# Router and low-rank columns appended to the weight blocks, all seven products joint, weight sums kept in DRAM

## The chip, the cores and the metric

One core of one Trainium2 chip runs the whole kernel. The metric is the device time of one execution in microseconds (us), the median of several runs. TensorE (PE in the profile) multiplies, VectorE is DVE, ScalarE is ACT, GpSimd is POOL, and SyncE (SP) issues every DMA of this kernel from one queue, in order.

## The reference

`x` is 8 batches of 1024 tokens with 1024 features, all float32.

```python
x = x + xattn(layernorm(x), ctx, mask)     # ctx: 64 memory rows per batch
x = x + ffn(layernorm(x), W, lora_A, lora_B, router_w)

def ffn(h, ...):                           # 8 experts, rank 16, top 2
    base   = h @ W.T                       # 1024 x 1024
    logits = h @ router_w.T                # 8 columns
    w      = top-2 softmax of logits, spread over 8 experts
    Ax     = h @ lora_A                    # 8 * 16 = 128 columns
    return base + 2.0 * ((Ax * w) @ lora_B)
```

So each token needs the 1024 x 1024 product, 136 more columns of the same input (128 low-rank, 8 router), a top-2 choice among 8 logits, and a product of 128 x 1024 that depends on that choice.

## The kernel before

The 8192 tokens are 64 tiles of 128, taken as 32 *pairs* (256 tokens); two pairs make a *quad*. `first()` handles pairs 0 and 1, loads the weights and forms sums of them; then `quad(u)` runs for u = 2, 4, ..., 30. Inside `quad(u)`, u and v = u + 1 are the pairs in the feed-forward part, n and m the two pairs after these (attention and layer norm, to be ready for the next quad), f and g the two after those (scores). Every engine's order is the order in which the Python code emits instructions; nothing reorders it.

The 1024 x 1024 product of a pair is done with Strassen's scheme (in Winograd's form): rows of the pair in two tiles, columns and contraction in halves of 512, seven products instead of eight. Product 1 is plain (`product(u, 1)`, 4 matmuls of 512 columns). The other six are *joint* for u and v: `joint(i, u)` applies the scheme once more, with quarter blocks of 256 columns (weights' quarter sums `q2, q3, q4` stay in SBUF; operand sums `s1..s4` come from `joint_sums`, L775 to L785, on POOL). One joint has seven blocks of two matmuls. Results are added from PSUM into `xt` (the residual, in SBUF) by DVE, helper lines L818, L692. Product 6 goes through a tile `hA`, which POOL adds into `xt` three times (`six_add`, L747).

The 136 extra columns are matmuls of their own: `rt_low_rank_tile`, 8 matmuls of 136 columns per tile (tile `pa`, L578). `rt_top` (L591 to L612) picks the two experts on DVE and weights the 128 low-rank columns; `rt_turn_low_rank` transposes them (`trw`, L621) and copies them with ACT (L623); then `lora` adds `axwt @ lb` (L695), in the same PSUM bank as the products.

Attention of a pair: `att_scores` (tile `sct`, L412), `att_sc` (transposition), `att_shift` and `att_exp` (softmax; `att_divide` normalizes it), `att_turn_p` (`ptp`), `att_readout` (`ro`, L480), `att_add`. Layer norm of the result: `f_sums` (L243), `f_squares` (L253), `f_std` (L261), `f_rows` (L291 to L296, writes `h`), `norm_send` (to DRAM and back in a blocked layout, `hd`, `hs`), `rt_turn_tile` (DVE 32 x 32 transposes into `hA`, `hB`), `rt_sums` (POOL).

A piece of work is placed between blocks of a joint by *hooks*: `hooks[k]` is emitted after the k-th block. An engine's queue is in order, so an instruction that waits holds up everything behind it on its engine.

Of the kernel before, what the change touches and what calls it, by code (L numbers as in the profile page):

```python
# [24 lines left out]
def kernel(  # L25
# [34 lines left out]
    HH = HB // 2  # L60

    const = ctx.enter_context(tc.tile_pool(name="const", bufs=1))
    xpool = ctx.enter_context(tc.tile_pool(name="xpool", bufs=10))
    ring = ctx.enter_context(tc.tile_pool(name="ring", bufs=5))
# [30 lines left out]

    def load_xs(u: int, tiles=(0, 1)):

        for r in tiles:
            xs = ring.tile([P, 4, QD], F32, tag="ring", name=f"xs_{u}_{r}")
            load_blocked(xs, xf[(2 * u + r) * P : (2 * u + r + 1) * P, :])  # L100
            xss.setdefault(u, []).append(xs)

    def load_xt(u: int):
        xts[u] = []
        for r in range(2):
            xt = xpool.tile([P, D], F32, tag="xt", name=f"xt_{u}_{r}")
            nc.sync.dma_start(out=xt, in_=xf[(2 * u + r) * P : (2 * u + r + 1) * P, :])
            xts[u].append(xt)
# [9 lines left out]
    art_sb = const.tile([P, KD, ER + E], F32, name="art_sb")  # L118
    art_v = ar_t.rearrange("(q k i) c -> q i k c", q=4, i=NB)
    wt_v = w_t.rearrange("(q k i) o -> q i k o", q=4, i=NB)  # L120
    blk = {}

    def load_w(kh: int, oh: int):
        w = const.tile([P, KH, HB], F32, name=f"w{kh + 1}{oh + 1}")
        for q in range(4):
            nc.sync.dma_start(
                out=w[q * NB : (q + 1) * NB, :, :],
                in_=wt_v[q][:, kh * KH : (kh + 1) * KH, ts(oh, HB)],
            )
        blk[kh + 1, oh + 1] = w  # L130
# [14 lines left out]
    for q in range(4):  # L145
        nc.sync.dma_start(out=art_sb[q * NB : (q + 1) * NB, :, :], in_=art_v[q])
# [13 lines left out]
    iota_e = const.tile([P, 2, E], F32, name="iota_e")  # L160
# [4 lines left out]
    def mask_bias(b: int):  # L165

        biases[b] = memp.tile([P, M], F32, tag="bias", name=f"bias_{b}")
        nc.vector.tensor_copy(biases[b], masks.pop(b))
        valids[b] = memp.tile([P, 1], F32, tag="valid", name=f"valid_{b}")
        nc.vector.tensor_reduce(valids[b], biases[b], AX.X, ALU.max)  # L170
        nc.vector.tensor_scalar(biases[b], biases[b], NEG, -NEG, ALU.mult, ALU.add)
# [9 lines left out]
    def row_stats(mv, src, name: str, parts: int = P):  # L181
        st = small.tile([P, D // HB, 6], F32, tag="st", name=f"st_{name}")
        for c in range(D // HB):
            nc.vector.bn_stats(st[:parts, c, :], src[:, ts(c, HB)])
        nc.vector.bn_aggr(mv, st[:parts])
# [3 lines left out]
    def x_sums(u: int, tiles=(0, 1)):  # L189
# [4 lines left out]
        for r in tiles:  # L194
            nc.scalar.activation(  # L195
                nowhere, xts[u][r], AF.Identity, accum_out=sm[:, r, :]
# [4 lines left out]
    def x_squares(u: int):  # L201
        nm, ss = stds[u][:, 0], stds[u][:, 1]
        for r in range(2):
            nc.scalar.activation(  # L204
                nowhere, xts[u][r], AF.Square, bias=nm[:, r, :],
# [27 lines left out]
    junk = const.tile([P, D], U8, name="junk")  # L233
    nowhere = junk
# [3 lines left out]
    def f_sums(u: int):  # L238
# [3 lines left out]
        for r in range(2):  # L242
            nc.scalar.activation(  # L243
                nowhere, xts[u][r], AF.Identity, accum_out=sm[:, r, :]
# [4 lines left out]
    def f_squares(u: int):  # L249
        nm, of_f = fts[u]  # L250
        ss = of_f[:, 2]
        for r in range(2):
            nc.scalar.activation(  # L253
                nowhere, xts[u][r], AF.Square, bias=nm[:, r, :], accum_out=ss[:, r, :]
# [9 lines left out]
    def f_rows_steps(u: int):  # L264
# [4 lines left out]
        def row(r: int):  # L269
# [3 lines left out]
                h, xts[u][r], AF.Identity, bias=nmr[:, r, :], scale=rstd[:, r, :]  # L273
# [13 lines left out]
    def f_rows(u: int, fetch: bool = True):  # L287
# [5 lines left out]
        for r in range(2):  # L293
# [3 lines left out]
                h, xts[u][r], AF.Identity, bias=nmr[:, r, :], scale=rstd[:, r, :]  # L297
# [4 lines left out]
    def blocked(src):  # L302

        return src.rearrange("p (q k i) -> p k q i", q=4, i=NB)
# [8 lines left out]
    def centre_mem(b: int, chunks: bool):  # L313
# [7 lines left out]
        mc = ring.tile([P, D], F32, tag="ring", name=f"memc_{b}_{chunks}")  # L321
# [20 lines left out]

    def load_ms(b: int):

        msr = ring.tile([P, D], F32, tag="ring", name=f"ms_{b}")
        n = M // NB * QD
        ms = msr[:, :n].rearrange("p (t c) -> p t c", c=QD)
        load_blocked(ms, mem[b])
        ones = msr[:, n : n + P]
        nc.gpsimd.memset(ones, 1.0 / D)  # L350
        mcs[b] = ms, ones, msr[:, n + P : n + P + M]

    def turn_mem(b: int):

        mt = memp.tile([P, KD, M], F32, tag="memT", name=f"memT_{b}_True", bufs=1)
        ms, ones, of_k = mcs[b]
        transpose_blocked(mt, ms)
        nc.vector.tensor_reduce(of_k, mt.rearrange("p k m -> p m k"), AX.X, ALU.add)
        mem_ts[b, True] = mt

    def centre_turned(b: int):

        _, ones, of_k = mcs.pop(b)
# [6 lines left out]
    x_ts, scs, ps, pts, ros, hds, hss = {}, {}, {}, {}, {}, {}, {}  # L370

    def transpose_pe(parts, src, name: str, later: bool = False):

        copies = []
        for c in range(2):
            v = bank_of(f"tr_{name}_{c}").rearrange("p (k i) -> p k i", i=P)
            for k in range(KH):
                nc.tensor.transpose(v[:, k, :], src[:, ts(c * KH + k, P)], ident)
# [5 lines left out]
    def xT_tile(u: int, r: int):  # L384
        t = ring.tile([P, KD, P], F32, tag="ring", name=f"xT_{u}_{r}")
        x_ts.setdefault(u, []).append(t)
# [6 lines left out]
    def att_turn_tile(u: int, r: int):  # L393
        transpose_blocked(xT_tile(u, r), xss[u][r])
# [5 lines left out]
    def att_scores(u: int, apart: bool = False):  # L400
# [4 lines left out]
        mt = mem_ts[u // PPB, u > 1]  # L405
        if apart:
            sct = bank_of(f"sct_{u}")[:, :P]
        else:
            sct = ps_at.tile([2 * M, P], F32, tag="at", name=f"sct_{u}")
        for k in range(KD):  # L410
            for r in range(2):
                mm(  # L412
                    sct[r * M : (r + 1) * M, :], mt[:, k, :], x_ts[u][r][:, k, :],
                    start=(k == 0), stop=(k == KD - 1),
                )
        scs[u] = small.tile([2 * M, P], F32, tag="tp", name=f"scts_{u}", bufs=2)
        nc.scalar.copy(scs[u], sct)
# [6 lines left out]
    def att_sc(u: int):  # L424
        sc = ps_at.tile([P, 2, M], F32, tag="at", name=f"sc_{u}")
        nc.tensor.transpose(sc.rearrange("p j m -> p (j m)"), scs.pop(u), ident)
        scs[u] = sc

    def att_shift(u: int):

        b, rstd, sc = u // PPB, sts.pop(u), scs.pop(u)
        s = small.tile([P, 2, M], F32, tag="s", name=f"s_{u}")
        for r in range(2):
            nc.vector.scalar_tensor_tensor(
                s[:, r, :], sc[:, r, :], rstd[:, r, :], biases[b], ALU.mult, ALU.add
            )
        of_s = small.tile([P, 3, 2], F32, tag="of_s", name=f"of_s{u}")
        mx, den = of_s[:, 0], of_s[:, 1]
        nc.vector.tensor_reduce(mx, s, AX.X, ALU.max, negate=True)
        ps[u] = s, of_s  # L440

    def att_exp(u: int):
        if u not in ps:
            att_shift(u)
        s, of_s = ps[u]
        mx, den = of_s[:, 0], of_s[:, 1]
        for r in range(2):
            nc.scalar.activation(
                s[:, r, :], s[:, r, :], AF.Exp, bias=mx[:, r : r + 1],
                accum_out=den[:, r : r + 1],  # L450
            )

    def att_divide(u: int):
        s, of_s = ps[u]
        den, rden = of_s[:, 1], of_s[:, 2]
        nc.vector.reciprocal(rden, den)
        tt(s, s, rden.unsqueeze(2).to_broadcast([P, 2, M]), ALU.mult)
        ps[u] = s

    def att_turn_p(u: int, in_place: bool = False):  # L460
        if in_place:
            ptp = ps_rt.tile([2 * M, P], F32, tag="rt", name=f"ptp_{u}")
        else:
            ptp = ps_at.tile([2 * M, P], F32, tag="at", name=f"ptp_{u}")
        s = ps.pop(u).rearrange("p j m -> p (j m)")
        nc.tensor.transpose(ptp, s, ident)  # L466
        if in_place:
            pts[u] = s
        else:
            pts[u] = small.tile([2 * M, P], F32, tag="tp", name=f"pt_{u}", bufs=2)  # L470
        nc.scalar.copy(pts[u], ptp)
# [10 lines left out]

    def att_add_tile(u: int, r: int):
        for c in range(NH):
            add(u, ros.pop((u, c, r)), r, c)
# [20 lines left out]
    def norm_rows(u: int, r: int, here: bool):  # L506
# [15 lines left out]
        nc.scalar.activation(h, xts[u][r], AF.Identity, bias=nmr, scale=rstd)  # L522
# [17 lines left out]
    has, hbs, pas, axls, axwts, sms = {}, {}, {}, {}, {}, {}  # L540

    def h_tiles(u: int):
        has[u] = turned.tile([P, 2, KH, P], F32, tag="hA", name=f"hA_{u}")
        hbs[u] = []

    def hb_tile(u: int, r: int):
        if r == 0:
            h_tiles(u)
        t = turned.tile([P, KH, P], F32, tag="hB", name=f"hB_{u}_{r}", bufs=5)
        hbs[u].append(t)  # L550
        return t

    def rt_turn_pe(u: int, r: int):
        hb = hb_tile(u, r)
        transpose_pe((has[u][:, r], hb), hss[u][r], f"h{u}_{r}")

    def rt_turn_tile(u: int, r: int):
        hb = hb_tile(u, r)
        half = KH * NB
        for t, c in ((has[u][:, r], 0), (hb, half)):  # L560
# [6 lines left out]
    def rt_low_rank(u: int):  # L567

        for r in range(2):
            rt_low_rank_tile(u, r)  # L570

    def rt_low_rank_tile(u: int, r: int, midway=None):
        if r == 0:
            pas[u] = ps_rt.tile([P, 2, ER + E], F32, tag="rt", name=f"pa_{u}")
        pa = pas[u]
        for k in range(KD):
            h = has[u][:, r, k, :] if k < KH else hbs[u][r][:, k - KH, :]
            mm(pa[:, r, :], h, art_sb[:, k, :], start=(k == 0), stop=(k == KD - 1))  # L578
            if midway and k == KH:
                midway()  # L580
        if r == 1:
# [773 lines left out]
```

## Time and profile before

| | |
|---|---|
| median of 3 runs (lowest, highest) | 1103.32 us (1103.19, 1104.22) |
| the profiled execution | span 1101.5 us |
| busy | PE 1090.6, DVE 819.8, ACT 556.2, POOL 567.1 us |
| data moved | 174.01 MB, 158 GB/s |
| DMA engines' share of the span | 50.3% |

Busy times are sums over one profiled execution. A matmul's record has a modelled end, so the cost of a matmul in a stream is read as the distance between starts. One float32 matmul of the program appears as two MATMUL records. The granted TensorE clock is full over the whole span.

### The profile page before, as it was taken

How to read it: one execution, taken by the hardware profiler on the slowest of the kernel's cores; microseconds unless marked ns; L12 is line 12 of the kernel's file. 1: busy time of each engine (PE TensorE's matmuls, PEld its weight loads, DVE VectorE, ACT ScalarE, POOL GpSimd, SP SyncE). 2: the span in 40 equal slices, each digit the busy share in tenths (PEclk: the TensorE clock that was granted, in tenths of full speed). 3: DMA queues.
4: the chain of work that ended last, by engine and by line, in shares of the span. 5: the costliest groups of instructions: out<-in, count | busy, mean ns of one | idle time of the engine just before them, and what ended most of it. 6: DMA issues, size and time to landing. Idle time of an engine off the chain costs nothing.

```text
span 1101.5 us, 17562 instructions
## 1 busy us (share of the span) xinstructions
PE 1090.6 (99%) x5864; PEld 846.6 (77%) x5864; DVE 819.8 (74%) x2069; ACT 556.2 (50%) x1063; POOL 567.1 (51%) x629
## 2 busy tenths in 40 slices
PE   8999999999999999999999999999999999999998
PEld 6555787887878788787787878878787787877877
DVE  6666977769777687867869778687777778667665
ACT  4577363727539173573726638174472735636010
POOL 0079563635647265373644646356372644647372
PEclk9999999999999999999999999999999999999999
DMA  9857446363474625646265473635636355432301
GB/s 229 212 181 218 137 154 217 100 200 125 153 230 131 211 82 193 197 148 199 101 196 152 153 230 100 195 118 190 203 135 193 108 203 147 153 115 91 139 1 77
DMA packets 104921, 174.01 MB, mean 158 GB/s; under 512 B 12928, under 2 KB 77440, under 8 KB 104832
## 3 DMA queue, kind: packets, MB, share of 16 engines
q1 hardware_dynamic: 104832, 172.90, 50.3%
q8 instruction: 47, 0.77, 0.3%
q14 instruction: 42, 0.34, 0.1%
HBM read 107.84 MB, written 65.01 MB: 157 GB/s over the span
## 4 chain that ended last, share of the span: by engine, by line
PE 95%; DVE 2%; POOL 1%; ACT 1%; DMA 1%; SPq 0%; issue 0%; DVEq 0%; ACTq 0%; POOLq 0%
PE jl L703 28%; PE ju L703 21%; PE pa L578 10%; PE ch L703 9%; PE ro L480 5%; PE sct L412 5%; PE ju L695 4%; PE jl L695 3%; PE plain L703 3%; PE ch L695 2%; PE j L703 1%; DVE xT L89 1%; PE trw L621 1%; DMA xs<-in_x_dram 1%; PE ptp L466 1%; SPq L83 0%
## 5 line engine op out<-in xcount | busy, mean ns | idle before, releaser
L818 DVE TENSOR_TENSOR xt<-jl,xt 128x256 f32<-128x256 f32 x421 | 191.6, 485 | 139.6 <-PE jl L703 90.8
L818 DVE TENSOR_TENSOR xt<-ju,xt 128x256 f32<-128x256 f32 (+1 forms) x210 | 110.7, 551 | 56.2 <-PE ju L703 52.6
L635 POOL TENSOR_TENSOR s<-hA,hB 128x512 f32<-128x512 f32 x31 | 39.7, 1280 | 208.4 <-PE jl L703 92.9
L747 POOL TENSOR_TENSOR xt<-xt,hA 128x512 f32<-128x512 f32 x90 | 111.4, 1275 | 29.1 <-DVE hA L814 29.1
L195 ACT ACTIVATE junk<-xt 128x1024 uint8<-128x1024 f32 x60 | 63.2, 1053 | 123.6 <-DMA xt<-in_x_dram 123.1
L703 PE MATMUL ch<-w,hA 128*128 128x512 f32 x248 | 113.7, 593 | 0.0
L642 POOL TENSOR_TENSOR hA<-hA 128x512 f32<-128x512 f32 x31 | 39.6, 1277 | 139.8 <-PE pa L578 139.8
L703 PE MATMUL ju<-w,s_j 128*128 128x256 f32 x360 | 94.7, 385 | 0.2
L703 PE MATMUL ju<-t,s_j 128*128 128x256 f32 x360 | 92.7, 380 | 1.4 <-ACT hA L810 0.9
L692 DVE TENSOR_TENSOR xt<-ch,xt 128x512 f32<-128x512 f32 x124 | 81.3, 678 | 9.6 <-PE ch L703 4.5
L296 ACT ACTIVATE h<-xt,of_f 128x1024 f32<-128x1024 f32 x60 | 71.2, 1232 | 22.9 <-DVE of_f L292 14.1
L692 DVE TENSOR_TENSOR xt<-ro,xt 128x512 f32<-128x512 f32 x128 | 79.6, 676 | 3.7 <-PE ro L480 3.7
L703 PEld LDWEIGHTS ju<-t,s_j 128*128 128x128 f32 x360 | 66.2, 190 | 18.1 <-issue 5.3
L703 PEld LDWEIGHTS ch<-w,hA 128*128 128x128 f32 x248 | 44.7, 190 | 42.7 <-issue 41.8
L703 PE MATMUL jl<-t,s 128*128 128x256 f32 x300 | 76.0, 384 | 0.0
L703 PEld LDWEIGHTS ju<-w,s_j 128*128 128x128 f32 x360 | 63.9, 190 | 15.7 <-issue 6.8
L89 DVE STREAM_TRANSPOSE xT<-xs 128x1024 f32<-128x1024 f32 x60 | 73.6, 1229 | 0.6
L578 PEld LDWEIGHTS pa<-art_sb,hA 128*128 128x128 f32 x512 | 66.3, 190 | 9.8 <-issue 8.6
L578 PE MATMUL pa<-art_sb,hA 128*128 128x136 f32 x512 | 70.0, 280 | 0.0
L204 ACT ACTIVATE junk<-xt,of_x 128x1024 uint8<-128x1024 f32 x60 | 68.9, 1149 | 2.0
L578 PE MATMUL pa<-art_sb,hB 128*128 128x136 f32 x512 | 69.8, 279 | 0.0
L253 ACT ACTIVATE junk<-xt,of_f 128x1024 uint8<-128x1024 f32 x60 | 69.0, 1149 | 1.5
(202 smaller groups left out, 2425.0 us busy)
## 6 DMA issues: line engine op xcount, KB each, us to landing
xt<-in_x_dram SPq DMA_DIRECT2D x64, 512.0 KB, 4.8
out_dram<-xt SPq DMA_DIRECT2D x62, 512.0 KB, 3.0
xs<-in_x_dram SPq DMA_DIRECT2D x240, 128.0 KB, 4.1
hd<-h SPq DMA_DIRECT2D x60, 512.0 KB, 2.7
hs<-hd SPq DMA_DIRECT2D x240, 128.0 KB, 3.0
mem<-in_ctx_dram SPq DMA_DIRECT2D x16, 256.0 KB, 3.6
w<-in_w_t_dram SPq DMA_DIRECT2D x16, 256.0 KB, 10.0
ms<-in_ctx_dram SPq DMA_DIRECT2D x28, 64.0 KB, 2.0
```

Source lines behind the costliest of these rows:

```text
L89: nc.vector.transpose(dst.rearrange("p k (t i) -> p t k i", i=NB), src.rearrange("p t (k i) -> p t k i", i=NB),)
L195: nc.scalar.activation(nowhere, xts[u][r], AF.Identity, accum_out=sm[:, r, :])
L204: nc.scalar.activation(nowhere, xts[u][r], AF.Square, bias=nm[:, r, :], accum_out=ss[:, r, :],)
L253: nc.scalar.activation(nowhere, xts[u][r], AF.Square, bias=nm[:, r, :], accum_out=ss[:, r, :])
L296: nc.scalar.activation(h, xts[u][r], AF.Identity, bias=nmr[:, r, :], scale=rstd[:, r, :])
L412: mm(sct[r * M : (r + 1) * M, :], mt[:, k, :], x_ts[u][r][:, k, :], start=(k == 0), stop=(k == KD - 1),)
L578: mm(pa[:, r, :], h, art_sb[:, k, :], start=(k == 0), stop=(k == KD - 1))
L692: tt(xc, bank, xc, ALU.add)
L695: mm(bank, axwts[u][:, r, :], lb_sb[:, c0 : c0 + n], start=alone, stop=True, skip_group_check=True)
L703: mm(bank, a[:, k, :], w[:, k, :], start=(start and k == 0), stop=(k == n - 1), skip_group_check=True)
L747: nc.gpsimd.tensor_tensor(xc, xc, t_of(u), ALU.add)
L818: tt(xc, src, xc, ALU.add)
```

## The change

- **Columns.** Each weight block `w11..w22` becomes `[128, 4, 2, 290]`: to each half of 256 columns 34 of the 136 extra columns are appended (`HX = 256 + 34`; `weight_low_rank` copies them in with ACT). The sums of weights are formed over 290 columns. `xt` gets the same layout, with 34 columns behind each quarter, which `x_zero` sets to zero. The logits and low-rank products then appear in these columns at the end of the quad; `rt_low_rank_tile` is left for pairs 0 and 1 and the last quad.
- **A period later.** `route` (choice of experts), `turn_low_rank` and `lora` of pairs a = u - 2, b = u - 1 are done in `quad(u)`, with banks of their own (`lora_tile`), and then the pair is stored.
- **All seven joint.** `product(u, 1)` becomes `joint(1, u)`; the order is 2, 5, 4, 1, 6, 7, 3. Products 1, 5, 6, 7 are collected in tiles `T` (SBUF), which POOL adds into `xt` (`t_add`).
- **Quarter sums of weights** go to DRAM once; `fetch` brings three pieces per joint into 4 buffers.
- Also: xs tiles are transposed in place, exp of both pairs together, the division by the softmax sum moves into the readout's add (`ro_add`), `xpool` 10 to 12 buffers, `ring` 5 to 4.

```diff
-    def rt_sums(u): # POOL: s1, s2, s4
+    def sums_1_2(u): # POOL: s1 = hA[1] + hB[1]; s2 = s1 - hA[0]
+    def sum_4(u):    # POOL: s4 = hB[0] - s2
+    def fetch():
+        name, i = wanted.pop(0)
+        nc.sync.dma_start(out=piece(name, i), in_=kept[name][:, i - 2])
+    def t_add(r, c, *pairs, wide=HX):
+        for p in pairs:
+            xc = xts[p][r][:, 2 * c : 2 * c + 2, :wide]
+            nc.gpsimd.tensor_tensor(xc, xc, Ts[p][:, :, :wide], ALU.add)
     def att_exp(pairs):
...
+        nc.vector.reciprocal(rden, den)
     def turn_low_rank(*pairs):
+        trw = ps_rt.tile([ER, n, P], F32, tag="rt", ...)
+        for j, u in enumerate(pairs):
+            for i in (2 * j, 2 * j + 1):
+                nc.tensor.transpose(trw[:, i, :], axl[:, i, :ER], ident)
+            nc.scalar.copy(axwt[:, two], trw[:, two])
     def joint(i, u, hooks, wide=HX, copy=None):
+        def read(p, k, bank):   # copy into T if fresh, else DVE adds the bank to T or xt
...
+        part(chain, a[:, :HK], b11, True);  hook(0); read(u, 0, chain); hook(1)
+        part(p4, d[:, HK:], q4, True);      fetch(); read(v, 0, p4);    hook(2)
+        part(p5, s1, q1, True);             read(v, 1, p5);             hook(3)
+        part(chain, s2, q2, False);         fetch(); read(u, 1, chain); hook(4)
+        part(p2, a[:, HK:], b21, True);     read(u, 0, p2);             hook(5)
+        part(p5, s4, b22, False);           read(u, 1, p5);             hook(6)
+        part(chain, s3, q3, False);         fetch()
+        tt(to(v), chain.unsqueeze(1).to_broadcast([P, 2, wide]), to(v), ALU.add)
     def quad(u):
+        att_sc([n, m]); ...  hooks[1] = att_exp([n, m]); hooks[3], hooks[5] = att_turn_tile(g, 0), (g, 1)
+        joint_sums(5, u); joint(2, u, hooks, wide)
+        sum_4(u); sum_4(v); sum_3(u); sum_3(v); joint_sums(4, u)
+        low_rank_gather(a, b); att_turn_p([n, m]); route(a, b); att_scores([f, g])
+        att_readout(n); att_add(n); att_readout(m); att_add(m); x_zero(n, m)
+        f_sums(n); f_squares(n); f_std(n)
+        turn_low_rank(a, b)
+        joint(5, u, {1: f_rows(n)}, wide, vector)
+        f_sums(m); f_squares(m); f_std(m); f_rows(m)
+        joint_sums(1, u); t_add(0, 1, u, v); t_add(1, 1, u, v)
+        lora_tile(a, r); store(a, r)                       # r = 0, 1
+        joint(4, u); joint_sums(6, u); lora_tile(b, r); store(b, r); load_xt(f)
+        joint(1, u, {}, wide, scalar); t_add(0, 0, u, v); joint_sums(7, u); x_stats(f); load_xt(g)
+        joint(6, u, {1: rt_turn_tile(n, 0), 4: rt_turn_tile(n, 1)})
+        joint_sums(3, u); sums_1_2(n); t_add(0, 1, u, v); load_xs(f + 2)
+        joint(7, u, {1: rt_turn_tile(m, 0), 4: rt_turn_tile(m, 1)})
+        x_stats(g); load_xs(g + 2); sums_1_2(m); joint_sums(2, n); t_add(1, 0, u, v); t_add(1, 1, u, v)
+        joint(3, u, {1: att_turn_tile(f + 2, 0), 4: att_turn_tile(f + 2, 1)})
```

(The new `quad` is shown with its calls on fewer lines and its conditions for the last quads left out.)

## The prediction

> **What bounds the kernel now.** I read the page first, then the waits of PE, the windows of single quads, and the timelines of the engines in one steady quad.
>
> ```profile
> PE 1090.6 (99%) x5864; PEld 846.6 (77%) x5864; DVE 819.8 (74%) x2069; ACT 556.2 (50%) x1063; POOL 567.1 (51%) x629
> ```
>
> A modelled busy share could hide gaps, so the waits of PE (total us, times, longest) and a steady quad (u = 16; busy us of PE, PEld, DVE, ACT, POOL) decide:
>
> ```profile
> PE ptp L466 <- DVE s L457: 1.0, 1, 1.0
> PE ju L703 <- ACT hA L810: 0.9, 1, 0.9
> 574.10:640.40 66.30, 66.30 (x365) 52.75 (x365) 50.69 (x130) 36.08 (x68) 34.62 (x38) 1.00 0.53 166
> ```
>
> PE waits about 8 us in the whole run, none of it in a steady quad: TensorE's stream is the time, and every matmul taken out is gain as long as no new wait appears. Its prices are distances between starts (start, us, form, records):
>
> ```profile
> 574.14 3.60 PE L703 MATMUL ch<-w,hA 128*128 128x512 f32 x8
> 577.58 0.59 PE L695 MATMUL jl<-lb_sb,axwt 128*128 128x256 f32 x2
> 578.01 1.09 PE L578 MATMUL pa<-art_sb,hA 128*128 128x136 f32 x8
> 578.94 1.09 PE L578 MATMUL pa<-art_sb,hB 128*128 128x136 f32 x8
> ...
> 592.32 3.71 PE L412 MATMUL sct<-xT,memT_True 128*64 128x128 f32 x64
> 595.96 1.99 PE L480 MATMUL ro<-mem,s 64*128 64x512 f32 x8
> ...
> 602.52 1.03 PE L703 MATMUL ju<-t,s_j 128*128 128x256 f32 x4
> 603.38 1.03 PE L703 MATMUL jl<-t,s 128*128 128x256 f32 x4
> ```
>
> Two records are one matmul: 512 columns cost 3.44 / 4 = 0.86 us, 256 cost 0.432, 136 cost 0.93 / 4 = 0.232; scores of two pairs 3.64, a readout 1.92.
>
> **PE's work.** Before, per quad: 84 x 0.432 (six joints) + 8 x 0.86 (product 1) + 32 x 0.232 (low rank) + 12 x 0.432 + 2 x 0.86 (lora) + 3.64 + 3.84 + 1.2 (small transposes) = 66.2, the 66.3 of the window. After: 290 columns lie on the line between 256 and 512, 0.432 + 34 x 0.00167 = 0.489 (bounds 0.432 and 0.86). A joint is 14 x 0.489 = 6.84. 7 x 6.84 + 8 x 0.86 (lora) + 3.64 + 3.84 + 1.2 = 63.5. So the edit is worth 2.8 us a quad if PE stays fed. That is little, and the new order of the program decides the rest. These rows price it:
>
> ```profile
> 602.77 1.28 ACT L261 ACT_TABLE_LOAD   x1
> 604.06 0.29 ACT L261 ACTIVATE of_f<-of_f,eps_sb 128x2 f32<-128x2 f32 x1
> ...
> 613.30 1.06 ACT L243 ACTIVATE junk<-xt 128x1024 uint8<-128x1024 f32 x1
> ...
> 618.45 0.30 ACT L261 ACTIVATE of_f<-of_f,eps_sb 128x2 f32<-128x2 f32 x1
> ```
>
> From the first sum of a pair to its standard deviation ACT takes 613.30 to 618.75 = 5.45 us, and 1.28 more where Exp's table was loaded before.
>
> ```profile
> 582.33 0.24 DVE L591 MAX8 top<-axl 128x8 f32<-128x8 f32 x2 [0.43 <-ACT axl L583]
> ...
> 584.48 0.49 DVE L612 TENSOR_TENSOR axl<-axl,we 128x128 f32<-128x128 f32 x2
> ...
> 593.54 2.46 DVE L692 TENSOR_TENSOR xt<-ro,xt 128x512 f32<-128x512 f32 x4
> ```
>
> Routing of two tiles: 2.65 us. An add of 512 columns from PSUM: 0.60 in a row; the same reading gives 0.34 for 256, so 0.37 for 290 and 0.67 for 580.
>
> ```profile
> 605.55 7.43 POOL L747 TENSOR_TENSOR xt<-xt,hA 128x512 f32<-128x512 f32 x6 [1.63 <-DVE hA L814]
> ...
> 619.73 0.73 POOL L783 TENSOR_TENSOR s_j<-s_j,s 128x256 f32<-128x256 f32 x1
> 620.54 0.73 POOL L784 TENSOR_TENSOR s_j<-s,s_j 128x256 f32<-128x256 f32 x1
> 621.23 0.74 POOL L785 TENSOR_TENSOR s<-s,s 128x256 f32<-128x256 f32 x1
> ```
>
> POOL: 512 elements 1.24 each (1.36 where one needs the last), 256 elements 0.81 or 0.69; `t_add` over 580 then 1.39 (bounds 1.24, and 1.60, the longest 512 row).
>
> **Wait 1, before joint 5, the largest.** `turn_low_rank` transposes four tiles into one bank: two, an ACT copy, two more. In ACT's queue that copy stands behind `f_std(n)`; in PE's queue the third transpose stands ahead of joint 5. So from joint 2's last matmul this chain must end before joint 5 starts: DVE's last read of joint 2, late by 1.5 us (wait 2 and two xs transposes of 1.16 inside the joint); `route` of four tiles 5.0 (between 4.0, where only its per-tile operations double, and 5.3, all doubled); two readout adds 1.2; f_sums to f_std 5.45 + 1.28 = 6.7; the copy 0.35 (L623); handovers 0.15; two transposes 0.2. Sum 15.1. PE has 3.64 + 3.84 + 0.9 = 8.4 to do meanwhile: **6.7 us waited**. Bounds: with the least lag and 4.0 for routing 13.4, so 5.0; with 5.3 and dearer POOL contention 16.5, so 8.1. Who waits behind it: everything on PE.
>
> The Trainium skill ("ScalarE: Activation LUTs", What ACT_TABLE_LOAD costs) adds a drain of 1.38 us to each 1.28 us load; the trace has the next ACTIVATE 1.29 after the load's start, so nothing is added here. By the page wait 1 would be 8.1.
>
> The skill also speaks against the change's shared bank ("PSUM — Partial Sum Buffer", PSUM bank collisions raise a hardware error): engines are to be kept apart by bank and quadrant, not by address, so other columns of the bank are no way round the copy. No run here shows a collision; without the rule wait 1 would shrink to nothing more than the PE work.
>
> **Wait 2, inside joint 2.** After the first read DVE does the shift (4 x 0.20 + 0.4), ACT four exps at 0.36, then DVE's reciprocal of their sums, all ahead of reads 2 to 7. First read done 1.6 after the joint's start, exps done 4.4, reciprocal 4.6, third read 5.4, but block 6 is due at 4.9 and needs it: 0.6. Then an xs transpose stands ahead of the fourth read, 7.0, and block 7 is due at 6.5: 0.6. **1.2** (0.5 to 2.2).
>
> **Wait 3, joint 7.** `t_add(0, 1)` reads T; joint 7's first read adds to T, so it waits for POOL. POOL's queue from joint 6's end: two sums of `joint_sums(3)` 0.81 + 0.69 (they need joint 6's last operand buffer), `sums_1_2(n)` 1.36 + 1.3, `t_add(0, 1, u)` 1.39, start 0.2: 5.75; DVE's read and handover 0.45: 6.2. Block 4 overwrites that bank and is due at 3 x 2 x 0.489 = 2.9: 3.3 waited, and 0.1 more behind the h transposes: **3.4** (2.9 to 4.5).
>
> **Wait 4, joint 4.** The reciprocal of pair m's deviation stands ahead of the lora adds and joint 4's reads on DVE, and `h` of n and two fetches must pass SP, whose `hs` issues took 3.64 us for 8. Both come out within half a us of need: **0.5** (0 to 2).
>
> Quad: 63.5 + 6.7 + 1.2 + 3.4 + 0.5 = **75.3**, 9 more than before.
>
> **What lies beside it.** POOL per quad: 28 x 0.75 + 8 x 1.3 + 12 x 1.39 + zeroing 1 = 49; DVE about 51 as before (two readings cancel); both under 75, so neither bounds on the whole. Fetches add 21 x 297 KB a quad, 93 MB in all, to 174 MB: about 215 GB/s over the new span, where the first slice of the page had 229. An issue of 512 KB takes SP 0.75 us, so SP's queue has about 42 of 75 us. Four pieces are ahead; if this cover were gone each joint would wait up to a DMA's landing, 3 to 5 us. Operations that the trace lacks, all off PE: the readout add with a scale (as 0.60; 0.37 to 1.2), exps with PSUM operands (0.2 to 0.5), in-place xs transposes (1.16; 0.6 to 2.5). Scores read 32-element runs: 3.64 as now, at most double, of which the wait before joint 5 covers part: 0 to 2 a quad; nothing suggests a gain.
>
> **Other parts.** The first part ends at 104.95 (first matmul of quad 2). It takes over one pair's scores, 1.9, and POOL's sums grow from 24 of 1.24 to 28 of 1.39, near the end of its chain: 110 (107 to 118). Quad 2 took 70.1; it has no lora or routing of earlier pairs, 56.2 of work, but waits 3.4 in joint 2 (two more xs transposes), 3.8 for `f_std` of n and m, 3.4 in joint 7: 66.8. Quads 4 to 28: 13 x 75.3 = 978.9 (before: 175.04 to 1038.0, 863.0). The last quad, 63.5 before: 98 x 0.432 + 7.4 + 16 x 0.86 + 0.9 = 64.3, routing of u and v ahead of joint 4's reads 3.3, 0.5, end 2.5: 70.6. Sum 1226.3, against the profiled 1101.5; the median stood 1.8 above that span: **1228 us**.
>
> **Rivals.**
> - *The waits are hidden, PE stays the bound* (faster). One mechanism: ACT reaches the second pair's copy before PE needs it, so that with it the whole chain fits. Then 107 + 56.2 + 13 x 63.5 + 67 + 1.8 = **1057**. It decides below 2.8 us of waits a quad. For it: PE has 8.4 us of its own there, and before showed no wait. Against: even with free routing, readout n comes 4 us after joint 2, and the ACT rows alone then take 8. 6%.
> - *Only wait 1 is real*, as T is free in time and DVE catches up: 75.3 - 5.1 = 70.2, 13 x 5.1 less: **1162**. For it: POOL has 31 us free in the old quad. Against: its queue is in order and each row in it needs the one before. 13%.
> - *The fetches bind*: pieces late by 1 us in each joint, +7 a quad: **1319**. For it: SP's queue waits for landed `hd` and stores ahead of fetches. Against: 1.5 joints of lead. 6%.
> - *The extra columns cost more than the line*, 0.55 a matmul: +6 a quad where PE binds, about 1280. 2%.
> - My forecast: 73%.
>
> **Numbers.** A quad between 71.2 and 78.5 is -53 to +42 over 13, the ends above add some: the range is 1165 to 1272. Faster 0.06, same 0.01 (within 0.2%, 2.2 us, about what a measurement of this kernel can tell), slower 0.93.
>
> **What would show it.** Right: PE idle some 7 us ahead of joint 5 in each quad, ended by ACT's copy of `trw`; a stop in joint 7 at its fourth block ended by DVE after POOL's T add; two short ones in joint 2; 290-column matmuls 0.489 apart. Wrong: a quad near 63.5 without idle PE, or PE waiting for DMA pieces.

## The result, and the profile after

The changed kernel takes **1384.9 us** (median of 4 runs, 1374.1 to 1388.5) against 1103.7 before: a ratio of 1.253, 95% interval 1.248 to 1.258. The direction was forecast, the size was not: 281 us more instead of 125, and the time lies outside the range. The profiled execution took 1374.1 us, its span is 1372.2.

The page after, the lines on the engines, the granted clock, the DMA engines and their queue:

```profile
PE 1151.1 (84%) x4968; PEld 791.7 (58%) x4968; DVE 787.5 (57%) x1829; ACT 555.9 (41%) x1116; POOL 761.7 (56%) x837
...
PEclk9998898998999999899899999989999899889999
DMA  9889483966839569394874839658395783827534
...
q1 hardware_dynamic: 218352, 273.26, 67.2%
```

PE is no longer busy for 99% of the span but for 84%, the row of the clock, all 9 before, has an 8 in 10 of its 40 slices, and 273 MB pass the queue where 173 did. The waits of PE (total us, times, longest us):

```profile
PE trw L703 <- ACT axwt L704: 75.0, 15, 5.7
PE jc L801 <- DVE T L912: 44.5, 14, 3.2
PE jc L801 <- DMA q_w<-q_w: 40.2, 15, 3.7
PE jc L801 <- DMA q_t<-q_t: 10.8, 7, 6.4
```

The first two are the forecast's waits 1 and 3; the other two are waits for the fetched quarter sums of weights (the *pieces*, `q_w` and `q_t`), which it had as a rival. The quad u = 14, from its matmul `ptp` to the next quad's, and three stretches of it (columns: stretch, its length, busy us of PE, PEld, DVE, ACT and POOL, granted clock, DMA share, GB/s):

```profile
554.40:636.29 81.89, 69.51 (x302) 48.39 (x301) 48.16 (x114) 35.67 (x71) 46.96 (x53) 0.92 0.68 211
563.80:569.50 5.70, 0.00 (x0) 0.00 (x0) 2.92 (x7) 5.53 (x10) 0.00 (x0) 0.57 0.36 92
569.50:575.50 6.00, 5.99 (x15) 4.42 (x16) 1.16 (x4) 2.83 (x4) 0.00 (x0) 0.56 0.09 31
580.00:610.00 30.00, 27.57 (x96) 18.78 (x95) 15.95 (x30) 10.89 (x20) 15.22 (x17) 0.94 0.98 318
```

The clock falls to 0.57 while PE waits before joint 5 and is still 0.56 in the 6 us after it, with PE busy the whole time; from 580 to 610 the DMA engines are full. The same quad on PE's timeline:

```profile
563.36 0.44 PE L703 MATMUL trw<-ident,axl 128*128 128x128 f32 x2
569.51 0.69 PE L703 MATMUL trw<-ident,axl 128*128 128x128 f32 x2 [5.72 <-ACT axwt L704]
569.99 2.14 PE L801 MATMUL jc<-w,s 128*128 128x290 f32 x4
571.93 2.14 PE L801 MATMUL j<-q_t,s 128*128 128x290 f32 x4
573.86 1.62 PE L801 MATMUL j<-w,s_j 128*128 128x290 f32 x4
575.32 1.14 PE L801 MATMUL jc<-q_t,s_j 128*128 128x290 f32 x4
...
598.46 2.03 PE L801 MATMUL jc<-q_w,s_j 128*128 128x290 f32 x4 [2.42 <-DMA q_w<-q_w]
600.28 2.06 PE L801 MATMUL j<-w,hA 128*128 128x290 f32 x4
602.17 1.14 PE L801 MATMUL j<-w,s_j 128*128 128x290 f32 x4
...
617.27 1.25 PE L801 MATMUL jc<-q_t,s_j 128*128 128x290 f32 x4 [3.21 <-DVE T L912]
618.36 1.14 PE L801 MATMUL j<-t,hA 128*128 128x290 f32 x4
```

Four records are two matmuls; undisturbed blocks start 0.98 apart. Behind the 5.72 us of wait 1 the first three blocks of joint 5 take 1.94, 1.93 and 1.46; behind the 2.42 us for a piece of w11 two take 1.82 and 1.89; behind the 3.21 us in joint 7 here nothing is lost.

**The account.** Taking from PE's rows of 12 steady quads (215.80 to 1221.66) the waits, and what blocks take over their usual distance, gives in us a quad:

| part | forecast | measured |
|---|---|---|
| PE's work, undisturbed | 63.5 | 64.3 |
| wait 1 (gates, before joint 5) | 6.7 | 5.7, and 0.4 in the readout before it |
| wait 2 (joint 2) | 1.2 | 0.5 |
| wait 3 (joint 7, T) | 3.4 | 3.2 |
| pieces, and wait 4 | 0.5 | 3.4 |
| slow blocks behind waits | 0 | 6.3: 2.6 after wait 1, 2.1 after joint 1's piece, 1.2 after wait 3, 0.4 elsewhere |
| quad | 75.3 | 83.8 |

In all: the first part ends at 128.4 (110 forecast), quad 2 takes 79.5 (66.8), the 13 quads 1086.0 (978.9), the last quad with its tail 78.3 (70.6).

### The profile page after: what moved, and what is told of

Its sections match the earlier page's. It is cut to its first block, busy times and chain, and to the rows that moved or that the text cites. A ratio compares the mean times of both kernels' runs of the same rounds, so it can differ in the third digit from the quotient of the medians.

```text
span 1372.2 us, 16976 instructions
## 1 busy us (share of the span) xinstructions
PE 1151.1 (84%) x4968; PEld 791.7 (58%) x4968; DVE 787.5 (57%) x1829; ACT 555.9 (41%) x1116; POOL 761.7 (56%) x837
## 4 chain that ended last, share of the span: by engine, by line
PE 46%; DMA 16%; DVE 11%; POOL 11%; ACT 9%; issue 3%; SPq 3%; DVEq 0%; ACTq 0%; POOLq 0%
PE j L801 20%; PE jc L801 18%; PE lo L791 7%; DMA q_w<-q_w 5%; DMA q_t<-q_t 5%; POOL xt L839 3%; ACT junk L296 3%; DVE xt L544 3%; DMA xt<-in_x_dram 2%; SPq L85 2%; DMA xs<-in_x_dram 2%; DVE xt L912 1%; DVE xs L448 1%; ACT junk L286 1%; POOL s L716 1%
## 5 line engine op out<-in xcount | busy, mean ns | idle before, releaser
L839 POOL TENSOR_TENSOR xt<-xt,T 128x580 f32<-128x580 f32 (+1 forms) x180 | 247.9, 1406 | 193.3 <-DVE T L912 193.3
L801 PE MATMUL jc<-q_t,s_j 128*128 128x290 f32 (+1 forms) x480 | 144.0, 423 | 60.6 <-DVE T L912 44.5
L801 PE MATMUL jc<-q_w,s_j 128*128 128x290 f32 (+1 forms) x360 | 115.4, 447 | 43.3 <-DMA q_w<-q_w 40.2
L801 PE MATMUL j<-w,s_j 128*128 128x290 f32 (+1 forms) x480 | 143.2, 422 | 8.2 <-DVE xt L912 6.5
L801 PEld LDWEIGHTS jc<-q_t,s_j 128*128 128x128 f32 x480 | 92.0, 197 | 98.1 <-DVE T L912 54.3
L801 PEld LDWEIGHTS j<-w,s_j 128*128 128x128 f32 x480 | 95.9, 202 | 43.1 <-POOL s_j L876 10.4
L801 PE MATMUL j<-t,s_j 128*128 128x290 f32 (+1 forms) x360 | 108.0, 424 | 0.0
L791 PE MATMUL lo<-lb_sb,axwt 128*128 128x512 f32 x240 | 107.8, 592 | 0.0
L544 DVE SCALAR_TENSOR_TENSOR xt<-ro,of_s,xt 128x512 f32<-128x512 f32 x128 | 86.2, 743 | 6.1 <-PE ro L538 5.9
L788 DVE TENSOR_TENSOR xt<-lo,xt 128x512 f32<-128x512 f32 x120 | 79.1, 685 | 12.4 <-PE lo L791 8.3
```

Of the source, the lines that this page charges most:

```text
L544: nc.vector.scalar_tensor_tensor(xc, halves(ros.pop((u, c, r))), rdens[u][:, r : r + 1], xc, ALU.mult, ALU.add)
L788: tt(xc, halves(bank), xc, ALU.add)
L791: mm(bank, axwts[u][:, r, :], lb_sb[:, c0 : c0 + n], start=alone, stop=True, skip_group_check=True)
L801: mm(bank, a[:, k, :], w[:, k], start=(start and k == 0), stop=(k == n - 1), skip_group_check=True)
L839: nc.gpsimd.tensor_tensor(xc, xc, Ts[p][:, :, :wide], ALU.add)
```

## The experiments

Theory: PE pays each wait twice, by its length and by the slow clock behind it, and the fetched sums fill the DMA engines in the middle of each quad. Rivals: another engine's chain sets the quad, so that a wait that is taken away shows elsewhere; and only the order in SP's queue makes pieces late. The kernels are compared with the changed kernel's 1384.9, whose own runs spread over 14 us.

**One wait at a time.** First, the copy of the gates:

```diff
             for i in (2 * j, 2 * j + 1):
                 nc.tensor.transpose(trw[:, i, :], axl[:, i, :ER], ident)
-            nc.scalar.copy(axwt[:, two], trw[:, two])
             axwts[u] = axwt[:, two]
+        nc.scalar.copy(axwt[:, :n], trw)
```

> All four transposes of the gates go into the bank first and one ACT copy of all follows, so PE no longer needs ACT ahead of joint 5. Theory (each wait of PE costs its own length and the slower matmuls behind it): the 5.72 us of wait 1 and the 2.5 us that joint 5's first three blocks lose are gone in 14 quads; the chain behind ACT's sums now shows in joint 5 (0.5 to 1.5 us, DVE's reciprocal waits for the root) and in joint 4 (1 to 3 us, the lora adds stand behind the second reciprocal); the wait for w11's pieces stays near 3. About 5 us a quad less: 1315 us, 1290 to 1335. Rival (ACT's and DVE's chain sets the quad, PE's wait is only where it shows): all of it comes back further on, 1365 or more. Rival (joint 5's first blocks are slow for a reason of their own): they stay at 1.94 apart with no wait ahead of them.

1349.4 us: half of the 70 expected. Wait 1 and its slow blocks are gone, but joint 5 now waits 1.6 us and joint 4 1.1 for DVE, and the waits for pieces rise from 51 to 72 us in all, with their slow blocks:

```profile
PE jc L801 <- DMA q_t<-q_t: 45.2, 20, 7.0
...
PE jc L801 <- DMA q_w<-q_w: 27.0, 11, 4.8
PE j L801 <- DVE T L910: 20.4, 13, 1.6
```

Of what was taken out most came back: 33 us of waits for DVE, 21 of waits for pieces, and the slow blocks behind those. Next, T:

```diff
         joint_sums(3, u)
+        t_add(0, 1, u, v, wide=wide)
         if more:
             sums_1_2(n)
-        t_add(0, 1, u, v, wide=wide)
```

> POOL adds T to the rows (0, 1) ahead of the two sums of pair n instead of behind them. Theory: joint 7's wait falls from 3.2 to about 0.7 us, and the slow blocks behind it, seen in 6 of 14 quads with 1.9 to 3.3 us, go with it: 14 x 2.5 + 12 = 47 us less, 1338 us, 1325 to 1352. Rival (POOL's queue is the limit there): the sums of n and m come later, joints 3 and 2 wait instead, less than 10 us gained.

1328.7 us, 56 less; joint 7's waits fall from 44.5 to 8.7 us in all, and only 9 us more of waiting for pieces take their place. POOL's order was the cause and POOL had room.

**Is it the clock?** `keep_warm(6, lb_sb[:, :HB])` ahead of the transposes of the second pair's gates:

> The wait before joint 5 stays as it is, but PE spends it on six idle matmuls of 512 columns (5.15 us) into a bank that nothing reads. Theory (the clock of TensorE falls because it waited): joint 5 starts at the same time, the wait shown is about 0.6 us, and its first blocks are 0.98 apart instead of 1.94, 1.94 and 1.4: 14 x 2.5 = 35 us less, 1350 us, 1338 to 1360. Rival (the blocks are slow from their operands, from DVE's copies or from DMA): 1385 us as before, the pitch still 1.94.

1362.3 us, 23 less (35 expected). PE's timeline:

```profile
551.27 5.32 PE L220 MATMUL idle<-lb_sb,ident 128*128 128x512 f32 x12
557.16 0.44 PE L705 MATMUL trw<-ident,axl 128*128 128x128 f32 x2 [0.57 <-ACT axwt L706]
557.43 1.14 PE L803 MATMUL jc<-w,s 128*128 128x290 f32 x4
558.41 1.14 PE L803 MATMUL j<-q_t,s 128*128 128x290 f32 x4
```

Joint 5 starts no earlier (PE comes to the third transpose 15.1 us behind ptp in both), has the same operands and transfers, and its blocks are 0.98 apart from the first on. So the slow blocks come from PE's own idleness. Of the 2.5 us some went into a new 0.83 before joint 4's fourth block and into waits for pieces. The same with `keep_warm(3, ...)`:

> The changed kernel with three idle matmuls of 512 columns at the start of the wait before joint 5 in place of six: PE then waits 5.72 - 2.6 = 3.1 us there. Theory (a longer wait costs more clock): the blocks behind it lose less than behind 5.72 us (2.5) and more than behind 0.6 us (0.2), on average about 1 to 2 us, as behind the waits of 2.4 to 3.6 us in joints 1 and 7. Rival (any wait of over 2 us costs the whole 2.5 us): 2.3 or more in every quad.

1370.3 us. The wait left is 3.14 us; in 8 of 12 quads not one block behind it is slow, in 4 they lose 1.3 to 1.7 us, 0.5 on average: less than expected, between 0.2 (wait 0.57) and 2.6 (5.72). One of the four:

```profile
1057.05 0.44 PE L705 MATMUL trw<-ident,axl 128*128 128x128 f32 x2 [3.14 <-ACT axwt L706]
1057.33 1.14 PE L803 MATMUL jc<-w,s 128*128 128x290 f32 x4
1058.31 1.99 PE L803 MATMUL j<-q_t,s 128*128 128x290 f32 x4
1060.09 2.03 PE L803 MATMUL j<-w,s_j 128*128 128x290 f32 x4
```

The first block runs at full speed and the two after it slow, so length alone does not settle when the clock falls. In the changed kernel, too, the 3.1 to 3.2 us in joint 7 cost clock in 6 of 14 quads, and 2.4 to 3.7 us in joint 1 in 12 of 13.

What tells these apart is in the traces' record of the granted clock. It is only ever whole or half (means between come from stretches that hold both), and in each trace of the changed kernel and its versions its changes lie whole multiples of 3.413 us apart, on a grid that is fixed within the run. Here are two steps of that grid from a quad of this run that paid nothing, and two from the quad above (columns as before):

```profile
635.20:638.61 3.41, 1.70 (x8) 1.42 (x9) 0.18 (x1) 2.01 (x4) 0.00 (x0) 1.00 0.00 0
638.61:642.03 3.42, 3.42 (x15) 2.66 (x14) 1.89 (x6) 2.81 (x3) 0.69 (x1) 1.00 0.23 92
1055.04:1058.45 3.41, 1.40 (x7) 1.18 (x8) 0.00 (x0) 2.31 (x6) 0.00 (x0) 1.00 0.00 0
1058.45:1061.87 3.42, 3.42 (x9) 2.40 (x8) 1.15 (x4) 2.50 (x3) 0.00 (x0) 0.50 0.14 55
```

The same 3.14 us leave PE busy for 1.70 of 3.41 us in the emptiest step in one case, and for 1.40 in the other, and the clock of the next step follows. So it is in the rest: in this run the four waits that paid left a step with PE busy for 0.15 to 0.41 of it, the eight that did not 0.42 to 0.53. In the changed kernel the waits in joint 7 that paid left 0.08 to 0.42 and the others 0.42 to 0.53; those in joint 1 that paid 0.04 to 0.37, the one other 0.52. What counts is how a wait falls on the grid. Busy time is not the whole measure: ahead of wait 1 in the changed kernel, behind the readout, the clock also fell after a step with PE busy for 0.71.

**Are the DMA engines full, or is SP's order wrong?** In the changed kernel the pieces of w11 go out at 593.05, behind hs of m and two stores, some 7 us after the buffer is free (SP's queue):

```profile
583.65 1.45 SPq L594 DMA_DIRECT2D hd<-h  x2
587.88 3.64 SPq L85 DMA_DIRECT2D hs<-hd  x8
591.62 1.33 SPq L950 DMA_DIRECT2D out_dram<-xt  x2
593.05 2.25 SPq L778 DMA_DIRECT2D q_w<-q_w  x2
```

First the order, with hs of m behind joint 4's pieces:

```diff
-            f_rows(m)
+            f_rows(m, False)
...
         joint(4, u, {}, wide)
+        if more:
+            norm_fetch(m)
```

> The eight fetches of pair m's turned h are issued behind joint 4's three pieces instead of ahead of them and of two stores. Theory (the piece of w11 is late because SP holds it behind the landing of hd, not because DMA is full): joint 1's wait (2.4 to 3.7 us) goes and with it the 1.7 to 3.0 us that its next blocks lose: about 5 us in 14 quads, 1315 us, 1300 to 1330. Rival (the transfers themselves bind): another joint waits for a piece instead, less than 20 us gained.

1390.7 us: nothing gained, the expectation is wrong by 75 us. Counted from ptp, the pieces of w11 go out 5.9 us earlier and joint 1 no longer waits, but the eight hs now take 8.02 us to issue instead of 3.64, and joint 6 waits for its piece:

```profile
588.04 2.40 SPq L778 DMA_DIRECT2D q_w<-q_w  x2
...
591.18 8.02 SPq L85 DMA_DIRECT2D hs<-hd  x8
...
603.17 1.64 SPq L778 DMA_DIRECT2D q_t<-q_t  x3
```

```profile
609.05 2.27 PE L801 MATMUL jc<-q_t,s_j 128*128 128x290 f32 x4 [5.60 <-DMA q_t<-q_t]
```

So order was not the whole of it. The run with the rows of x out of the crowd (`load_xt(f)` behind joint 1, `load_xt(g)` behind joint 6):

> As the run with pieces first (hs of m behind joint 4's pieces), and the rows of f and g are loaded one joint later each: f behind joint 1's pieces, g behind joint 6's. Theory (from joint 4 to joint 6 the DMA engines are full, 8.4 MB in 26 us at a share of 98%, so an issue moved ahead only delays what now comes behind it): with 2 MB out of that stretch's queue no piece is late by over 1 us in joints 1 and 6; 3.0 us of waiting and 2.0 of slow blocks are gone in 14 quads: 1315 us, 1300 to 1345. Rival (the sum of the transfers is too much for the quad): the wait moves to joint 7 or 3, less than 20 us gained.

1328.6 us, as expected: waits for pieces 23 us in all instead of 51.

**All waits of PE but DMA's**, then with DMA's. Besides the two edits above, `f_rows(n)` moves from joint 5's first to its fifth hook, and `f_rows(m)` into joint 4's fifth:

> The waits of PE that are not DMA's are taken out: one copy of the gates, T added ahead of the sums of n, and the two reciprocals of h later on DVE (behind joint 5's and joint 4's fifth reads); every DMA stays in its order, so that h of m and its fetch move later against joint 4's pieces. Without any cost of DMA 14 x (5.7 + 2.5 + 2.5 + 0.9) = 162 us would be gained: 1222 us. Theory (what is taken out ahead of joints 4 to 6 squeezes 8 MB of transfers into less time): pieces come later by 4 to 7 us a quad, 1290 us, 1265 to 1320, with the waits for pieces at 6 to 10 us a quad. Rival (SP's order and not the amount decides): the waits for pieces stay near 3 and the time is 1230 or less.

1294.4 us, close to the theory's number: of the 162 us that the sum takes out, 72 came back, as later pieces (100 us of waits for them instead of 51) and slow blocks. All of it, with `norm_fetch(m)` inside joint 1:

> All of it: one copy, T first, both reciprocals later, rows of f and g one joint later, hs of m issued inside joint 1 behind its first piece. Theory: PE has 64.5 us of work a quad, and of the waits some 2 us for pieces and 2 us of DVE are left: 69 a quad, 128 + 72 + 13 x 69 + 75 + 2 = 1175 us, 1150 to 1215. Rival (16.8 MB a quad are too much for a quad of under 75 us): 1250 us or more, pieces late in several joints.

1240.1 us: between theory and rival, outside the theory's range. A quad takes 74 us, with 64.3 of work. Its two halves (u = 14, columns as above):

```profile
586.40:600.00 13.60, 13.17 (x105) 8.96 (x104) 11.60 (x40) 7.19 (x16) 2.10 (x8) 1.00 0.28 60
600.00:658.58 58.58, 52.53 (x200) 36.69 (x199) 37.36 (x75) 27.28 (x54) 43.65 (x44) 1.00 0.94 277
```

The clock is whole in this quad (0.97 over the run, 0.92 in the changed kernel); the DMA engines are at a share of 0.28 while PE scores and reads out, and at 0.94 in the other 58.6 us. The estimate of 2 us for late pieces was too low. The same kernel without the stores:

> The version with all waits treated, without the stores of the finished rows of the earlier pairs in all quads but the last (those rows are left unwritten): 2 of 16.8 MB a quad less, in the stretch where the DMA engines are full, at no other change. Theory (the pieces are late because the DMA engines are full for 42 us of a quad): of 5 us waiting for pieces and 2 us of slow blocks most goes, 1240 - 13 x 5 = 1175 us, 1150 to 1200. Rival (the pieces wait for their turn behind xs in SP's queue, however much is moved): 1220 or more.

1201.5 us, 39 less for 2 MB a quad. That is just outside the range. The waits for pieces of t1 to t4 (q_t, 27.1 us in all) are gone; those of q_w, most of them in joint 3, stand. The stores' issues, 1.28 and 2.01 us of SP's time in the quad u = 14 with the stores, go too, so bytes and turns in the queue are not quite apart here. The waits with the stores and without:

```profile
PE jc L801 <- DMA q_w<-q_w: 43.9, 14, 4.4
PE jc L801 <- DMA q_t<-q_t: 27.1, 17, 3.1
```

```profile
PE jc L801 <- DMA q_w<-q_w: 41.2, 12, 4.7
```

Then the place in the queue, with the same bytes: of each pair of xs tiles the second is issued behind two pieces (`load_xs(f + 2, (1,))` in joint 7's fourth hook, `load_xs(g + 2, (1,))` in joint 3's):

> The version with all waits treated, and of the rows for the scores the second tile is issued behind two of joint 7's (joint 3's) pieces, the first ahead of them as before; the same bytes. Theory (the engines are full for 42 us, whatever the order): joint 3's wait (2.7 to 4.4 us and 1.9 of slow blocks) gets smaller, but DVE's transposes or the next pieces wait instead: 1232 us, 1215 to 1242. Rival (the order in the queue): joint 3's wait goes, none comes in its place: 13 x 5 = 65 us less, 1175 us, 1165 to 1190.

1221.4 us, 19 less, in the theory's range: joint 3's pieces come sooner (q_w 25.5 us in all), and DVE's adds behind transposes and POOL's sums hold PE up in some quads instead. Both together:

> The two ways of helping the pieces of joint 3 together: the stores of finished rows left out as in the run before of that kind (those rows stay unwritten), and the xs split around two pieces. Theory (volume and place both hold the pieces up: with less volume the pieces of joints 6 and 7 came in time, with the other place those of joint 3 came sooner): joint 3's wait of 2.7 to 4.7 us and the slow blocks behind it go in most quads, 13 x 4 = 52 us less than 1201: 1150 us, 1135 to 1170. Rival (the transfers' volume alone): no more than the 19 us that the split gave before: 1180 or more.

1194.4 us: only 7 less than without the stores, the rival's side. Pieces cost 28 us in all, and late xs and what waits for them take over. So the order mostly chooses whether pieces or xs are late, and bytes taken away make the lateness less. A queue of their own does not help (`nc.scalar.dma_start` in `fetch`):

> The version with all waits treated, with the pieces' fetches issued by ACT instead of SP, so that they stand in a queue of their own. Theory (the engines are full): the pieces come in time, hs, xs or x come later, and DVE's transposes or ACT's sums hold PE up instead: 1225 us, 1205 to 1240. Rival (only the order in SP's queue made them late): no wait for pieces and none in its place, 1170 or less. If ACT's own work suffers from the issues, it shows as later h and the time is over 1240.

1331.0 us, worse by 91 than from SP. That h of m goes out 3.7 us later, counted from ptp, is the smaller part. ACT is in order as well; its sums of f wait for x, and the pieces of joint 7 stand behind them:

```profile
662.81 0.34 ACTq L778 DMA_DIRECT2D q_t<-q_t  x1
675.05 1.06 ACT L239 ACTIVATE junk<-xt 128x1024 uint8<-128x1024 f32 x1 [14.40 <-DMA xt<-in_x_dram]
...
680.57 0.84 ACTq L778 DMA_DIRECT2D q_t<-q_t  x2
```

```profile
684.07 2.27 PE L801 MATMUL jc<-q_t,s_j 128*128 128x290 f32 x4 [11.52 <-DMA q_t<-q_t]
```

This run does not tell full engines from order, since the pieces were issued late.

**The first part.** `load_ms(1)` moves ahead of `f_rows(2)`, and `rt_turn(2)` and `att_turn(4)` behind `product_add(1, 7)`:

> Only the first part: the context of the second batch is loaded ahead of h of pair 2 and of the sums' stores, and two adds stand ahead of the transposes of h and x on DVE. Theory (the 18 us that the first part is late come from PE waiting on DVE, 5.5 and 2.8 us, and from the slow clock behind that): the first matmul of quad 2 comes at 120 instead of 128 us (116 to 125), the rest stays: 1377 us, 1365 to 1385. Rival (POOL's sums and their stores set the end of the first part): 127 or later.

The rival holds: quad 2 starts at 129.9, and nearly all the waits of the end of the first part have become one:

```profile
123.40 0.66 PE L469 MATMUL sct<-xs,memT_True 128*64 128x128 f32 x2 [15.80 <-DVE xs L448]
```

```profile
98.79 10.98 SPq L756 DMA_DIRECT2D q_t<-q_t  x6
109.86 0.88 SPq L594 DMA_DIRECT2D hd<-h  x2
...
116.67 3.76 SPq L85 DMA_DIRECT2D xs<-in_x_dram  x8
```

h of pair 3 goes out at 109.86 behind six stores of sums, for which POOL is not ready (10.98 us), and hs and xs follow it. With `quarter_sums("t3", t3)` moved behind `load_xs(5)`:

> As the run of the first part, and POOL's three sums of t3 with their stores come behind the load of xs of pair 5 in place of ahead of h of pair 3. Theory now (the end of the first part hangs on SP: h of pair 3, ready at 100.7, goes out at 109.9 behind six stores that wait for POOL, then hs, then xs of pair 5, and PE waits 15.8 us for that): h goes out some 8 us earlier and the first matmul of quad 2 comes at 120 instead of 130 (116 to 124); 1376 us, 1366 to 1386. Rival (another wait stands at the same place): 126 or later.

h goes out at 101.39, 8.5 us earlier as expected, but hs only at 108.37: it follows the issue of hd, on whose landing it waits, by 5.6 us where 2.3 passed before. In the two later versions with this order 5.4 and 5.5 pass, in all others 2.2 to 3.4; why is not shown. Quad 2 starts at 125.0, between theory and rival. Both kernels take 1391.6 us, no gain: 6.7 above the changed kernel's median and 3 above its slowest run. With all waits treated:

> The version with all waits treated, with the new first part. Theory: 8 to 10 us less than 1240: 1231 us, 1222 to 1238.

1239.4 us, outside the range and no gain against 1240.1: quad 2 starts 5.6 us earlier and gives part back. And everything that keeps the whole computation:

> Everything that keeps the whole computation: all waits treated, the new first part, xs split. Theory: the gains of the split (19 us) stand, the first part's 5 us are lost in quad 2 again: 1220 us, 1208 to 1226; still far above 1103, since the steady quad has 64.3 us of PE work and the transfers need about 50 us at full rate in the 58 us in which they can go.

1223.6 us. No version comes near before. An estimate from the rows of the version with xs split: 199.7 to the first joint matmul of quad u = 4, 13 quads of undisturbed work at 64.3 and the last at about the forecast's 70 make 1106 against the span of 1101.5 before. So even without a wait in a steady quad the change would only come about level while the start, which took 175.0 before, stays as it is. That sum is worked out, not run.

## Why the forecast was wrong

- **PE's work**: right. A matmul of 290 columns takes 0.489 us, on the line. The 0.8 more a quad is the second pair's readout, whose banks come free at DVE's pace.
- **Waits 1, 2 and 3**: right in place and nearly in size, 1 and 3 also in what releases them: 9.8 us where 11.3 was forecast. The chain ahead of joint 5 took the 15.1 us of the sum, and its terms came out too (DVE's lag 1.3, routing 5.15, sums to root 6.9); PE's own work meanwhile took 9.4 instead of 8.4. The runs with one copy and with T first confirm the releasers of waits 1 and 3. No run tests wait 2, whose second half the rows mostly put down to POOL's sum or to no releaser, not to DVE.
- **What follows a wait**: the term that failed most. The sum counted a wait as its length. The granted clock had been 1.00 in every slice of before, and so had no term. It is 6.3 of the 8.5 us missing in a quad, 5.1 of them by the clock's own record; the run with idle matmuls shows the cause for wait 1. The Trainium skill says it ("TensorE: Matmul & The Clock Gate", HAM oscillation: no idle gaps of over about 3.4 us, else the array goes back to half its clock), and the forecast did not use it. By that length wait 1 and three of joint 1's waits (3.5 to 3.7 us) would pay; here waits of 2.4 us paid too, and most of 3.1 to 3.2 in joint 7 did not, so the measurement decides: a few us waited may cost up to 3 more, by how they fall on the grid of 3.413 us.
- **Wait 4 and the rival that the fetches bind**: 0.5 forecast, 3.4 measured, plus 2.2 of slow blocks behind it. The bytes were right (274 MB forecast as 267), but their mean rate over the span was compared with a peak; in the stretch that matters, 580 to 610, the share is 0.98 and from 554 to 570 it is 0.20. The rival, priced at 1 us a joint, was right that pieces come late, and wrong in the place: one joint, not seven.
- **First part**: 110 forecast, 128.4 measured. "Near the end of its chain" was taken for nearly off the path. In the changed kernel six stores of sums hold SP from 98.9 to 108.2, and behind them stand h of pair 3, hs and xs. With three of them moved away quad 2 still started at 125.0, so what makes up the rest of the 18 us stays open.
- **Quad 2 and the end**: 12.7 and 7.7 more: joint 4 waits 6.4 us for a piece of t4 and loses 2.9 to the clock, joint 7 loses 1.9 more than its wait; in the last quad the tail behind PE took 6.2 us where 2.5 was taken.

## What to carry to other kernels

Where PE binds, price a new wait at its length plus what the clock loses behind it, and fill a wait that cannot be removed. An estimate from the grid above: a step of 3.41 us must lose about 2.0 us of PE's work (0.58 of it), so a lone wait well under 2 us costs no clock, one of over 4 us always does, and between them it is chance. The 17 traces of the changed kernel and its versions agree. Of the lone waits of 0.7 us and more ahead of a joint's block (no other near, the clock whole before) none of 163 under 1.8 us paid, 4 of 21 up to 2.0, 218 of 309 up to 4, and all 41 over 4. Ask of DMA not the mean rate but which stretch the transfers crowd into, and how full that one is; a change of order in a full stretch mostly chooses who waits (nothing gained with hs behind the pieces, 19 us with xs split), unless it moves transfers out of the stretch (56 us with the rows of x later). After removing waits one at a time, add up what the others gained: one copy took some 8 us a quad off the path and the quad got 2.5 shorter (35 us in 14 quads).

## What was not expected of the hardware

- The granted clock was 0.57 within a wait of 5.7 us and 0.56 for 6 us behind it; waits of 0.6 us left blocks at 0.98; 3.1 us cost 0 in 8 of 12 quads and 1.3 to 1.7 us in 4. The clock changes only on a grid of 3.413 us, and fell where a joint's wait left PE busy for less than about 0.42 of a step.
- Eight transfers that SP issues in 3.64 us at a DMA share of 0.63 take it 8.02 at a share of 0.91. That the crowd holds up the issuing engine is inferred from this, not tested alone.
